# Layer 1's group norm through DRAM, and image 1's attention half by half, in a four-layer hybrid kernel

## The chip, the cores and the metric

One core of a Trainium2 chip runs the whole kernel in one launch. The metric is the device time of an execution in microseconds. PE is TensorE (matmuls), DVE VectorE, ACT ScalarE, POOL GpSimd, and SP the sequencer that issues most DMAs. Each engine works through its own queue in the order in which instructions stand in it; semaphores tie the queues together.

## The reference, cut to what matters

The input x is (2, 256, 32, 32), float32: two images of 1024 positions with 256 channels. Four layers follow; the change concerns the first two and the seams behind them.

```python
# layer 0: group norm with 32 groups, then attention of all 2048 positions, 4 heads
x = x + conv_attn(gn(x, G=32))
# layer 1: mean and variance of a WHOLE image, then attention inside the image, 8 heads of 64
mu  = mean(x, axis=(1, 2, 3)); var = var(x, axis=(1, 2, 3))
xn  = (x - mu) * rsqrt(var + 1e-5) * gn_w + gn_b
q, k, v = split(w_in @ xn)
x = w_out @ softmax(q * 0.125 @ k.T) @ v + b_out + x
# layer 2: tokens; layer norm, window attention (64 tokens, shifted), then layer norm, top-2 of 8 experts
t = tokens(x); t = t + window_attn(ln(t)); t = t + experts(ln(t))
# layer 3: layer norm, additive attention sum_u wa[u] * tanh(q + k + bh), then layer norm, top-2 of 8 experts
```

## The kernel before, in words

The state `xT` lies in SBUF as channels by positions (128 partitions, 2 halves of the channels, 2048 positions).

`project0` makes layer 0's queries, keys and values in four quarters of 512 positions (t = 0 to 3). At t = 0 and t = 2 it takes an image's group norm first: `group_norm` runs `bn_stats` on DVE, and `pool_stats` averages over partitions with small matmuls (L542 here), twice, for the mean and for the variance. `rsqrt` is a chain of twelve tiny DVE operations (L131 to L138), with no table.

`front` runs layers 0 and 1. It makes a list of chunks and hands it to `attention`. A chunk is 512 query positions of one pair of heads. Layer 0 has 8 chunks of 64 steps, layer 1 has 16 of 8 steps: for each image four pairs of heads, and for each pair two halves t of the positions. One step handles 128 keys: four pairs of score matmuls (L215, L216), one exp on ACT (L218) into one of four `e` buffers, one addition on DVE (L224, L227) for the softmax's denominator, and eight matmuls with the values (L237). The order of the program is written out by hand: `attention` scores one or two steps ahead, and hangs further work on step numbers in `todo`: `divide` two steps after a chunk's end (L251 to L265: the sums over partitions, a reciprocal, and the product that goes to `oT`), the chunk's `finish` four or six steps after it, the next chunk's `prepare` four steps before its start, and `extras` where a chunk names them. A scheduler in the framework may then move an instruction within its engine's queue where dependences allow, so a place in the program is not yet a place in the queue.

Around the change the order is this. `norm(b)` is layer 1's group norm of image b: `group_norm` with matmuls against a constant 1/256 (L410), then four passes over the image on DVE for `xn`. `values` (L432, L436) and `heads` (L446, L450) project from `xn`; `heads(b, pair)` makes the queries and keys of a pair for all 1024 positions. For image 0 these stand in the extras of layer 0's second half, four steps apart from step 8 of its fifth chunk on; for image 1 they stand in the late chunks of image 0's layer 1. The last chunk of an image calls `output1(b)` (32 matmuls L457, additions to `xT` L463) and then `done(b)`: the positions are transposed to tokens (L1432), copied (L1435, L1437), and normalised by `norms`: statistics of eight tokens' tiles (L144, L145), one `rsqrt`, the scaling on ACT (L155), and `to_channels` (transposes L182, copies L184, L186). For image 0 that falls into image 1's first chunks; for image 1 it is followed by the window attention (projections L684, L689, L696, scores L711).

The experts of layer 2 (`mixture`: products L1130, L1154, transposes L1141, gelu L1146) are a generator, `second`, stepped one block at a time. Between it and the additive attention stands `prepare(0, ...)`, a generator that brings in the experts' results of image 0 for each token tile (DMAs L1200 on the SP and ACT queues, combination L1202), then layer-norms them and makes the additive attention's first operands (L1251). `second` is stepped beside it from its ninth item on.

Of the kernel before, what the change touches and what calls it, by code (L numbers as in the profile page):

```python
# [24 lines left out]
F32 = mybir.dt.float32  # L25
# [3 lines left out]
AF = mybir.ActivationFunctionType  # L29
ALU = mybir.AluOpType  # L30
# [3 lines left out]
P = 128  # L34
B, C, N = 2, 256, 1024
# [52 lines left out]
class Stack:  # L88
# [101 lines left out]
    def attention(self, chunks, pools):  # L190
# [94 lines left out]
        for n in range(at + 5):  # L285
            ahead = 2 if 0 < n < at and steps[n][1] == 0 else 1
            while scored < min(n + ahead + 1, at):
                score(scored)
                scored += 1
            if n < at:  # L290
                accumulate(n)
            for f in todo.pop(n, []):
                f()
# [39 lines left out]
    def front(self, xT, weights, tokens, done):  # L333
# [6 lines left out]
        with ExitStack() as ctx:  # L340
# [61 lines left out]
            whole = w1.tile([P, P], F32, name="whole")  # L402
            nc.gpsimd.memset(whole, 1.0 / C)
            xn, v, oT, q, k = {}, {}, {}, {}, {}

            def norm(b):

                mean, rs = self.group_norm(
                    w1, p_r, xT, b, lambda ps, rows: [
                        nc.tensor.matmul(  # L410
                            ps[:, o : o + 1], lhsT=whole, rhs=rows[:, c : c + 1],
                            start=(c == 0), stop=(c == CC - 1),
                        )
                        for o in range(CC) for c in range(CC)
                    ]
                )
                xn[b] = pools1[0].tile([P, CC, N], F32, name="xn")
                for c in range(CC):
                    nc.vector.tensor_scalar(
                        xn[b][:, c, :], xT[:, c, b * N : (b + 1) * N],  # L420
                        mean[:, c : c + 1], rs[:, c : c + 1], ALU.subtract, ALU.mult,
                    )
                    nc.vector.tensor_scalar(
                        xn[b][:, c, :], xn[b][:, c, :], gn_w[:, c : c + 1], gn_b[:, c : c + 1],
                        ALU.mult, ALU.add,
                    )
                v[b] = pools1[b].tile([P, N // P, HID], F32, name="v")
# [10 lines left out]
            def heads(b, pair):  # L438

                for part, to, scale in ((0, q, 0.125), (1, k, 1.0)):  # L440
                    to[b, pair] = two.tile([P, N], F32, name="qh" if part == 0 else "kh")
                    for t in range(N // CH):
                        ps = bank()
                        for c in range(CC):
                            at = part * HID + pair * P
                            nc.tensor.matmul(  # L446
                                ps, lhsT=w_in[:, c, at : at + P], rhs=xn[b][:, c, t * CH : (t + 1) * CH],
                                start=(c == 0), stop=(c == CC - 1),
                            )
                        nc.scalar.activation(to[b, pair][:, t * CH : (t + 1) * CH], ps, AF.Copy, scale=scale)  # L450

            def output1(b):
                for t in range(N // CH):
                    for o in range(CC):
                        ps = bank()
                        for c in range(PAIRS):
                            nc.tensor.matmul(  # L457
                                ps, lhsT=w_out[:, c, o * P : (o + 1) * P],
                                rhs=oT[b][:, c, t * CH : (t + 1) * CH],
                                start=(c == 0), stop=(c == PAIRS - 1),  # L460
                            )
                        x = xT[:, o, b * N + t * CH : b * N + (t + 1) * CH]
                        nc.vector.scalar_tensor_tensor(x, ps, b_out[:, o : o + 1], x, ALU.add, ALU.add)  # L463

            def chunk1(b, pair, t):
                def prepare():
                    if t == 0 and pair:
                        heads(b, pair)

                def finish():  # L470
                    if pair == PAIRS - 1 and t == N // CH - 1:
                        output1(b)
                        done(b, bank)

                def goes_to():
# [8 lines left out]
                    "q": lambda: q[b, pair][:, cols],  # L484
# [9 lines left out]
            chunks += [chunk1(b, p, t) for b in range(B) for p in range(PAIRS) for t in range(N // CH)]  # L494


            for b, at, first_step, apart in ((0, NCH, 8, 4), (1, NCH * CC + 5, N // P - 2, 1)):
                ready = [lambda b=b: norm(b), *(lambda b=b, i=i: values(b, i) for i in range(N // P))]
                ready += [lambda: None, lambda b=b: heads(b, 0)]
                for i, f in enumerate(ready):  # L500
                    step = first_step + apart * i
                    for c in chunks[at:]:
                        if step < c["n"]:
                            c.setdefault("extras", {}).setdefault(step, []).append(f)
                            break
                        step -= c["n"]
            self.attention(chunks, pools)

    def project0(self, pool, psum, xT, weights, to):
# [26 lines left out]
        for t in range(NCH):  # L536
            cols = slice(t * CH, (t + 1) * CH)
            if t % 2 == 0:
                b = t * CH // N
# [842 lines left out]
    def run(self):  # L1382
        tc, nc, ins = self.tc, self.nc, self.ins
        PER = N // P
        with ExitStack() as ctx:
            window = ExitStack()
            xw = window.enter_context(tc.tile_pool(name="wa_in", bufs=1, side="right"))
            with tc.tile_pool(name="xT", bufs=1, side="right") as xp:
# [19 lines left out]
                def norm(which, g, bank):  # L1408

                    tiles = slice(4 * g, 4 * g + 4)  # L1410
                    t, u, uT, mv = (have[n] for n in ("t", "u", "uT", "mv"))
                    rs = self.normalise(u[:, tiles], t[:, tiles], mv[:, which, tiles], 1e-5)
                    self.to_channels(uT[:, :, g * CH : (g + 1) * CH], u[:, tiles], bank)
                    return mv[:, which, tiles, 1], rs
# [12 lines left out]
                def done(b, bank):  # L1427

                    for i in range(b * PER, (b + 1) * PER):
                        ps = bank(0)[:, 0:C].rearrange("p (c d) -> p c d", c=CC)  # L1430
                        for c in range(CC):
                            nc.tensor.transpose(ps[:, c, :], xT[:, c, i * P : (i + 1) * P], self.ident)  # L1432
                        to = have["t"][:, i, :].rearrange("p (c d) -> p c d", c=CC)
                        if i % 2:
                            nc.scalar.copy(to, ps)  # L1435
                        else:
                            nc.vector.tensor_copy(to, ps)  # L1437
                    norms(0, b, bank)
# [126 lines left out]
            with ExitStack() as side:  # L1565
# [18 lines left out]
                for k, _ in enumerate(prepare(0, bank, enter(side, "outputs2"), PER, nc.sync, nc.scalar)):  # L1584
                    if k >= PER:
                        second.step()
# [45 lines left out]
class General(Stack):  # L1632
# [4 lines left out]
    def front(self, xT, weights, tokens, done):  # L1637
# [4 lines left out]
        with self.tc.tile_pool(name="tok_ps", bufs=4, space=PSUM) as psum:  # L1642
            for b in range(B):
                done(b, lambda k: psum.tile([P, CH], F32, name="tr"))
# [543 lines left out]
```

## Time and profile before

| | |
|---|---|
| three runs | 2504.87, 2511.28, 2515.06 us; median 2511.28 |
| the profiled execution | 2506.88 us, its span 2504.9, mean PE clock 0.978 |
| layer 0's projections | about 0 to 70 us of the span |
| layer 0's attention, 8 chunks | 70 to 1016 |
| layer 1, image 0 | 1016 to 1184 |
| layer 1, image 1, with image 0's output and layer norm | 1184 to 1352 |
| image 1's output and layer norm | 1352 to 1386 |
| window attention, routing, layer 2's experts | 1386 to 1710 |
| seam to the additive attention, then that attention | 1710 to 2245 |
| layer 3's experts | 2245 to 2505 |

The page of a profile lists busy time and instructions by engine, the chain of work that ended last, and groups of instructions as "line engine operation out<-in, shapes, count | busy us, mean ns of one | idle time before them and what ended most of it". A timeline lists instructions by start (us), duration (us), engine, line and operation; in brackets the engine's idle time before it and what it waited for. "x8" joins neighbours of the same kind.

### The profile page before, as it was taken

How to read it: one execution, taken by the hardware profiler on the slowest of the kernel's cores; microseconds unless marked ns; L12 is line 12 of the kernel's file. 1: busy time of each engine (PE TensorE's matmuls, PEld its weight loads, DVE VectorE, ACT ScalarE, POOL GpSimd, SP SyncE). 2: the span in 40 equal slices, each digit the busy share in tenths (PEclk: the TensorE clock that was granted, in tenths of full speed). 3: DMA queues.
4: the chain of work that ended last, by engine and by line, in shares of the span. 5: the costliest groups of instructions: out<-in, count | busy, mean ns of one | idle time of the engine just before them, and what ended most of it. 6: DMA issues, size and time to landing. Idle time of an engine off the chain costs nothing.

```text
span 2504.9 us, 42385 instructions
## 1 busy us (share of the span) xinstructions
PE 2350.2 (94%) x17211; PEld 1024.5 (41%) x17211; DVE 1701.1 (68%) x2616; ACT 1436.9 (57%) x1626; POOL 241.6 (10%) x254
## 2 busy tenths in 40 slices
PE   7999999999999999999999969997999988889997
PEld 4333333333333333333333536664444432334664
DVE  5677777775677777876578566326877788886543
ACT  1565556545555566544454333222999999999222
POOL 0000000000000000000001312221110000111342
PEclk9999999999999999999999989998999999999998
DMA  4000000000000000000000036775343202122896
GB/s 139 1 1 1 1 1 1 1 1 1 1 1 1 1 2 1 1 1 1 1 2 9 3 117 244 297 289 208 137 141 136 90 14 78 66 91 93 305 323 236
DMA packets 58928, 190.50 MB, mean 76 GB/s; under 512 B 14116, under 2 KB 28964, under 8 KB 48740
## 3 DMA queue, kind: packets, MB, share of 16 engines
q1 hardware_dynamic: 45236, 161.86, 18.3%
q0 software_dynamic: 8160, 22.29, 2.5%
q10 hardware_dynamic: 5328, 3.55, 0.5%
q8 instruction: 137, 2.24, 0.4%
q14 instruction: 67, 0.55, 0.1%
HBM read 168.15 MB, written 17.43 MB: 74 GB/s over the span
## 4 chain that ended last, share of the span: by engine, by line
PE 70%; DVE 11%; issue 7%; ACT 6%; DMA 3%; POOL 1%; SPq 0%; ACTq 0%; DVEq 0%; POOLq 0%
PE ps_o L237 20%; PE ps_t L215 19%; PE ps_e L1304 7%; PE bk_h L1130 4%; PE bk_y L1154 4%; ACT th L1295 3%; DVE sum L227 2%; PE ps_row L446 2%; PE ps_pt L1325 2%; DVE th L1285 2%; PE ps_qk L530 1%; PE ps_row L432 1%; DVE den L263 1%; DMA w<-in_l_w 1%; PE ps_row L457 1%
## 5 line engine op out<-in xcount | busy, mean ns | idle before, releaser
L227 DVE TENSOR_TENSOR sum<-sum,e 128x1024 f32<-128x1024 f32 x592 | 724.9, 1224 | 303.5 <-ACT e L218 292.6
L218 ACT ACTIVATE e<-ps_t 128x1024 f32<-128x1024 f32 x640 | 653.4, 1025 | 464.9 <-PE ps_t L216 463.4
L237 PE MATMUL ps_o<-e,v 64*64 64x512 f32 x5120 | 677.0, 592 | 8.5 <-DVE o L244 7.9
L215 PE MATMUL ps_t<-q,k 64*64 64x512 f32 x2048 | 533.0, 591 | 0.5 <-DVE v L571 0.5
L216 PE MATMUL ps_t<-q,k 64*64 64x512 f32 x2048 | 533.0, 591 | 0.0
L1285 DVE TENSOR_SCALAR th<-kT,qb 128x1024 f32<-128x1024 f32 x478 | 331.2, 749 | 90.2 <-PE ps_e L1304 87.9
L237 PEld LDWEIGHTS ps_o<-e,v 64*64 64x64 f32 x5120 | 194.1, 132 | 370.8 <-issue 179.4
L1295 ACT ACTIVATE th<-th 128x4096 f32<-128x4096 f32 x94 | 335.8, 3651 | 5.2 <-DVE th L1285 5.2
L1146 ACT ACTIVATE h<-bk_t,w 128x128 f32<-128x128 f32 x496 | 142.5, 375 | 267.2 <-issue 149.8
L1304 PE MATMUL ps_e<-th,pick 128*32 128x512 f32 x2048 | 270.2, 621 | 25.4 <-ACT p L1357 15.0
L215 PEld LDWEIGHTS ps_t<-q,k 64*64 64x64 f32 x2048 | 149.2, 133 | 287.2 <-issue 152.9
L1130 PE MATMUL bk_h<-w,xgT 128*128 128x512 f32 x496 | 242.9, 606 | 10.3 <-DVE xgT L1118 9.9
L1154 PE MATMUL bk_y<-w,h 128*128 128x256 f32 x992 | 247.9, 385 | 3.0 <-issue 1.0
L1154 PEld LDWEIGHTS bk_y<-w,h 128*128 128x128 f32 x992 | 178.3, 192 | 48.7 <-issue 24.0
L1135 DVE COPY hp<-bk_h 128x512 f32<-128x512 f32 x124 | 85.3, 688 | 121.6 <-PE bk_h L1130 121.5
L265 POOL TENSOR_TENSOR inverses<-inverses,den 128x512 f32<-128x512 f32 x24 | 30.5, 1269 | 1325.0 <-DVE den L263 1325.0
L216 PEld LDWEIGHTS ps_t<-q,k 64*64 64x64 f32 x2048 | 149.3, 133 | 0.0
L215 PE MATMUL ps_t<-qh,kh 64*64 64x512 f32 x512 | 139.4, 602 | 0.0
L216 PE MATMUL ps_t<-qh,kh 64*64 64x512 f32 x512 | 138.5, 600 | 0.0
L1304 PEld LDWEIGHTS ps_e<-th,pick 128*32 128x32 f32 x2048 | 58.3, 112 | 172.0 <-issue 115.2
L1161 POOL DMA_INDIRECT given<-y,gives x85 | 87.0, 1023 | 428.8 <-DVE y L1160 358.4
L1130 PEld LDWEIGHTS bk_h<-w,xgT 128*128 128x128 f32 x496 | 86.9, 193 | 80.8 <-issue 54.8
(335 smaller groups left out, 2053.6 us busy)
## 6 DMA issues: line engine op xcount, KB each, us to landing
w<-in_l_w SPq DMA_DIRECT2D x39, 1152.0 KB, 5.4
w<-in_l_w SPq DMA_DIRECT2D x39, 1030.0 KB, 7.0
w<-in_l_w SPq DMA_DIRECT2D x46, 640.0 KB, 6.7
w<-in_l_w SPq DMA_DIRECT2D x46, 514.0 KB, 5.4
rows<-u SPq DMA_DIRECT2D x8, 512.0 KB, 3.7
yt<-given SPq DMA_DIRECT2D x24, 128.0 KB, 2.3
k<-k SPq DMA_DIRECT2D x16, 128.0 KB, 2.2
uT<-given ACTq DMA_DIRECT2D x16, 128.0 KB, 4.1
```

The lines of the kernel that those rows point to most:

```text
L215: nc.tensor.matmul(ps[part, 0, :], lhsT=ka[:, part], rhs=q[0:64, :], start=True, stop=True)
L216: nc.tensor.matmul(ps[part, 1, :], lhsT=kb[:, part], rhs=q[64:128, :], start=True, stop=True)
L218: nc.scalar.activation(e, ps, AF.Exp)
L227: nc.vector.tensor_tensor(c["sum"], c["sum"], e, ALU.add)
L237: nc.tensor.matmul(c["po"][64 * r : 64 * r + 64, half, :], lhsT=v[part, :], rhs=e[part, r, :], start=(j == 0), stop=(j == c["n"] - 1),)
L1130: nc.tensor.matmul(ps, lhsT=inputs[b][:, c, :], rhs=first[b][:, at : at + CH], start=(c == 0), stop=(c == CC - 1),)
L1146: nc.scalar.activation(hidden[b, n][:, cols], ps[:, cols], AF.Gelu, bias=first[b][:, at : at + 1])
L1154: nc.tensor.matmul(sums[b], lhsT=h[:, j * P : (j + 1) * P], rhs=second[b][:, at : at + C], start=(n == 0 and j == 0), stop=(n == HH - 1 an ...
L1161: nc.gpsimd.indirect_dma_start(out=given[b], out_offset=index(slots(b)[1], b), in_=y, in_offset=None)
L1285: nc.vector.tensor_scalar(h[:, j, :], *keys_and_queries(n, j), None, ALU.add)
L1295: nc.scalar.activation(h, h, AF.Tanh)
L1304: nc.tensor.matmul(scored[i][U * j : U * (j + 1), a, :], lhsT=aa["pick"][:, m, :], rhs=h[:, j, a * CH : (a + 1) * CH], start=(m == 0), sto ...
```

## The change

Five edits. (1) Image b's group norm in layer 1 no longer uses matmuls. `look(b)` takes the statistics of each channel with `bn_stats`, stores them (128 x 4 numbers) to DRAM, and loads the whole row back into every partition, into the space of `v[b]`, which is not yet in use. `norm(b)` combines them there with `bn_stats` again. `look` stands in the program eight steps (image 0), and some chunks (image 1), ahead of `norm`. (2) Image 1's chunks run half by half: the four pairs for the first 512 positions, then the four for the second. Keys of all four pairs are kept, those of pairs 2 and 3 in the space of image 0's values. (3) `output1` and `done` work on 512 positions, and return lists of small steps that `attention` hangs on successive step numbers; the layer norm's scaling moves from ACT to DVE. (4) `project0` takes image 1's group norm at t = 1, not t = 2. (5) `second` is stepped once more, at `prepare`'s third item. The diff, cut to its core:

```diff
@@ attention
-        for n in range(at + 5):
+        n = 0
+        while n < at or todo:
...
             for f in todo.pop(n, []):
-                f()
+                for i, g in enumerate(f() or []):
+                    later(n + 1 + i, g)
+            n += 1
@@ front
+            def look(b):
+                st = w1.tile([P, CC, 2, 6], F32, name="gn_st")
+                mv = w1.tile([P, CC, 2], F32, name="gn_mv")
+                for c in range(CC):
+                    for i in range(N // CH):
+                        at = b * N + i * CH
+                        nc.vector.bn_stats(st[:, c, i, :], xT[:, c, at : at + CH])
+                    nc.vector.bn_aggr(mv[:, c, :], st[:, c])
+                rows = self.tc.dram_tile([P, CC * 2], F32, name=f"gn_rows{b}")
+                nc.sync.dma_start(out=rows[:, :], in_=mv.rearrange("p c s -> p (c s)"))
+                v[b] = pools1[b].tile([P, N // P, HID], F32, name="v")
+                every = v[b][:, 0, 0 : P * CC * 2]
+                nc.sync.dma_start(out=every, in_=rows[:, :].rearrange("p x -> (p x)").partition_broadcast(P))
+
             def norm(b):
-                mean, rs = self.group_norm(
-                    w1, p_r, xT, b, lambda ps, rows: [
-                        nc.tensor.matmul(
-                            ps[:, o : o + 1], lhsT=whole, rhs=rows[:, c : c + 1],
...
+                every = v[b][:, 0, 0 : P * CC * 2].rearrange("p (c s) -> p c s", s=2)
+                for i in range(2):
+                    nc.vector.bn_stats(st[:, i, :], every[:, :, i])
+                    nc.vector.bn_aggr(mv[:, i, :], st[:, i])
+                var = w1.tile([P, 1], F32, name="gn_var")
+                nc.vector.tensor_tensor(var, mv[:, 0, 1:2], mv[:, 1, 0:1], ALU.add)
+                mean, rs = mv[:, 0, 0:1], self.rsqrt(var, 1e-5)
...
+            def heads(b, pair, t):
+                for i in (t,) if b else range(0 if t else N // CH):
+                    q[b, pair, i] = two.tile([P, CH], F32, name="qh", bufs=4)
+                    project(b, pair, 0, i, q[b, pair, i])
+                if t:
+                    return
+                if b and pair >= 2:
+                    if not spare:
+                        spare.append(pools1[0].tile([P, N // P, HID], F32, name="v"))
+                    at = (pair - 2) * (N // CH)
+                    k[b, pair] = spare[0][:, at : at + N // CH, :].rearrange("p a d -> p (a d)")
+                else:
+                    k[b, pair] = two.tile([P, N], F32, name="kh")
+                for i in range(N // CH):
+                    project(b, pair, 1, i, k[b, pair][:, i * CH : (i + 1) * CH])
...
                 def finish():
-                    if pair == PAIRS - 1 and t == N // CH - 1:
-                        output1(b)
-                        done(b, bank)
+                    if pair == PAIRS - 1 and (b or t):
+                        follow = []
+                        for i in (t,) if b else (0, 1):
+                            follow += [lambda i=i, o=o: output1(b, i, o) for o in range(CC)]
+                            follow += done(b * (N // CH) + i, bank)
+                        return follow
...
-            chunks += [chunk1(b, p, t) for b in range(B) for p in range(PAIRS) for t in range(N // CH)]
+            chunks += [chunk1(0, p, t) for p in range(PAIRS) for t in range(N // CH)]
+            chunks += [chunk1(1, p, t) for t in range(N // CH) for p in range(PAIRS)]
...
-            for b, at, first_step, apart in ((0, NCH, 8, 4), (1, NCH * CC + 5, N // P - 2, 1)):
+            for b, looked, at, first_step, apart in ((0, (NCH, 8), NCH, 16, 4), (1, (NCH * CC, 12), NCH * CC + 5, N // P - 2, 1)):
+                due(*looked, lambda b=b: look(b))
@@ project0
-            if t % 2 == 0:
-                b = t * CH // N
+            if t < B:
+                b = t
@@ run
+                def token(i, bank):
+                    ps = bank(0)[:, 0:C].rearrange("p (c d) -> p c d", c=CC)
+                    for c in range(CC):
+                        nc.tensor.transpose(ps[:, c, :], xT[:, c, i * P : (i + 1) * P], self.ident)
...
+                    stats(0, i)
+
+                def done(g, bank):
+                    tiles = [lambda i=i: token(i, bank) for i in range(4 * g, 4 * g + 4)]
+                    return [*tiles, lambda: norm(0, g, None), *3 * [lambda: None], lambda: turns(g, bank)]
...
                 for k, _ in enumerate(prepare(0, bank, enter(side, "outputs2"), PER, nc.sync, nc.scalar)):
-                    if k >= PER:
+                    if k == 2 or k >= PER:
                         second.step()
```

`due(at, step, f)` hangs f on a step of a chunk, carrying over into later chunks. `norm(0, g, None)` is the layer norm of four token tiles, scaled on DVE (L160), and `turns` its `to_channels`.

## The prediction

> **What bounds the kernel now.** I read the page's busy shares first, then the chain that ended last, then tables of busy time by stage, then the timeline at the places that the diff touches. TensorE carries the kernel:
>
> ```profile
> PE 2350.2 (94%) x17211; PEld 1024.5 (41%) x17211; DVE 1701.1 (68%) x2616; ACT 1436.9 (57%) x1626; POOL 241.6 (10%) x254
> ...
> PE 70%; DVE 11%; issue 7%; ACT 6%; DMA 3%; POOL 1%; SPq 0%; ACTq 0%; DVEq 0%; POOLq 0%
> ...
> L227 DVE TENSOR_TENSOR sum<-sum,e 128x1024 f32<-128x1024 f32 x592 | 724.9, 1224 | 303.5 <-ACT e L218 292.6
> ```
>
> PE is busy 94%, so an edit pays only where it closes one of PE's few gaps; removed work on DVE or ACT pays nothing by itself. In the attention loop one step costs PE 1.72 us (the distance of two exps in a quiet stretch, 1109.39 to 1111.11), ACT 1.02, and DVE 1.22 for L227. DVE thus has only 0.5 us per step to spare: that is the resource to watch. The exps in the timeline show what image 0's norm costs:
>
> ```profile
> 531.53 1.02 ACT L218 ACTIVATE e<-ps_t 128x1024 f32<-128x1024 f32 x1 [0.69 <-PE ps_t L216]
> 539.26 1.02 ACT L218 ACTIVATE e<-ps_t 128x1024 f32<-128x1024 f32 x1 [6.71 <-PE ps_t L216]
> 542.47 1.02 ACT L218 ACTIVATE e<-ps_t 128x1024 f32<-128x1024 f32 x1 [2.18 <-PE ps_t L216]
> ```
>
> Two steps took 10.94 us instead of 3.44: 7.5 us lost. The table by stage (window, then PE, PEld, DVE, ACT and POOL busy, PE clock, DMA share, GB/s) shows the other places: image 0's output and layer norm inside image 1's first chunks (row 1), the tail before the window attention (row 2), and the gap ahead of the additive attention (rows 3 and 4):
>
> ```profile
> 1184.00:1230.00 46.00, 43.46 (x199) 16.36 (x198) 26.63 (x54) 16.16 (x26) 1.27 (x1) 0.93 0.00 0
> ...
> 1352.00:1386.50 34.50, 29.40 (x105) 14.54 (x106) 24.71 (x61) 10.72 (x22) 13.41 (x24) 0.95 0.11 17
> 1710.00:1720.00 10.00, 3.81 (x16) 2.29 (x14) 4.24 (x12) 0.37 (x1) 0.96 (x1) 0.81 0.64 203
> 1720.00:1730.00 10.00, 4.34 (x8) 2.05 (x9) 10.00 (x51) 2.03 (x7) 0.99 (x1) 0.50 0.58 195
> ```
>
> **What the Trainium skill says.** (1) "DMA: Bandwidth & Descriptors", Anatomy of one DMA: about 2 us of every DMA is fixed, mostly the receipt of the last write. The trace agrees: a 0.1 KB load takes 1.7 to 1.8 us to land, one of 128 KB 2.2 to 2.9. (2) "TensorE: Matmul & The Clock Gate", Part 1: an idle window drops PE to half clock until about 3.4 us of work have passed. The trace agrees: after the stall at 535 a score matmul took 1.06 us, not 0.59, until 541. (3) Same page, Architectural detail: DVE is strict FIFO, so an instruction waiting for a DMA holds all behind it. The trace has one such wait in the attention stages, 3.8 us of L797 on `sb_rel_pos` at 1311, and does not contradict it. (4) "SBUF — State Buffer", Who interferes with whom: a DVE instruction with two SBUF inputs contends with a GpSimd read. The trace agrees: between 1374 and 1379 eight tiny ops of `rsqrt` took 0.65 us each instead of 0.17 while POOL ran L647.
>
> **A. Image 0's norm.** Removed: 16 L410 matmuls over both images (0.97 us for eight, two lots per image) and the `gs` chain between. Added: `look` (same bn_stats), a store of 2 KB, a broadcast load of 256 KB, then bn_stats on the loaded rows and `rsqrt`, all DVE. Price of the exchange: 1.8 + 2.3 (an `out` store of 256 KB) plus two issues of 0.3 = 4.7 us; bounds 4.0 (1.7 + 2.2) and 6.2 (2.9 + 2.9 + issue). The program puts `look` eight steps ahead of `norm` (13.7 us), which would hide it. But in the built order of the queues the scheduler has moved `norm`'s first bn_stats up to only two L227 sums behind `look`'s last. Data ready at 532.3, landed near 537; DVE arrives there near 534.8 and waits some 2.3 us, with the sums queued behind it. `e` has four buffers, so the exps, and then PE, run dry: I count about 3.8 us of PE stall plus 1.2 of lowered clock. 7.5 - 5.0 = **2.5 gained**. Bounds: exchange at 4.0, 6 gained; at 6.2, 2 lost.
>
> **B. Image 1's norm.** Exps at 1111.11, 1116.71 and 1119.62 today: 5.07 us too much, 5.5 with the xn wait. Afterwards its statistics are taken at layer 1's first chunk near 1018, where `norm`'s wait is again pulled close behind. DVE then runs 4.7 us late, but there PE does 7.1 us of head projections and DVE idles 4.5 us, which hides it with about 1 us to spare. **5.5 gained**; 1 if the exchange takes 6.2 or that cover is thinner.
>
> **C. Image 1 half by half, layer norm in steps.** Today from the first L457 product of image 0 (1184.01) to the first window score (L711, 1386.06): 202 us, made of 168.5 to the last L251 (1352.47) and a tail of 33.6. Of the 168.5, PE has 151.7 of work: 60 steps x 1.72 = 103, L251 8, heads 21.2, output 13.9, transposes 5.6; the rest, 16.8, is stall.
>
> The tail's lines, with their waits:
>
> ```profile
> 1353.48 14.00 PE L457 MATMUL ps_row<-oT,sb_l_w_out 128*128 128x512 f32 x32
> 1354.44 3.36 DVE L263 RECIPROCAL den<-total 128x256 f32<-128x256 f32 x2 [0.69 <-ACT total L257]
> ...
> 1380.34 4.04 ACT L155 ACTIVATE u<-t,nm_shift,rs 128x256 f32<-128x256 f32 x8 [4.20 <-DVE nm_shift L153]
> 1380.99 0.33 PE L182 MATMUL ps_row<-ident,u 128*128 128x128 f32 x1 [3.01 <-ACT u L155]
> ```
>
> After: only half of the 32 L457 products, four tokens instead of eight. L251 to oT 7 us (as now, 1352.47 to 1359.49), last two products and add 1.7, four tokens at 1.0 (transposes 0.34, copy 0.41, bn_stats 0.42), `rsqrt` 12 x 0.19 = 2.3, L160 4 x 0.41 = 1.6, transposes and copies 2; with 1.4 of chunk ends, **20**. The window projection of image 0 (16 x 0.43 = 6.9) fills PE during this. Bounds: 18.5, and 26 if POOL's L647 adds fall on `rsqrt` again (12 x 0.48 more).
>
> The stretch before it grows. PE takes over 8.8 us from the tail (160.5). DVE now owes each group of four tokens about 9.5 us (copies 0.8, bn_stats and aggregates 2.4, `rsqrt` 2.5, L160 1.6, uT copy 0.7, output adds 1.5) over 15.2 per chunk (8 x 1.22, o copies, reciprocal 3.4, L264): 24.7 against 22.6 for a PE chunk with its heads. So DVE is just over PE: about 3 us in each of three groups, plus 3 once where the single `oT` buffer makes DVE's L264 wait for the products that still read it: stalls 12. 160.5 + 12 + 20 = 192.5; say 194 for clock loss. **8 gained**; bounds 14 (stalls halved) and 2 lost (DVE 5 us more per group).
>
> **D. project0.** The gap at 35.33 (PE waits 3.37 for xn, then 5.28 for eight matmuls instead of 3.43) is moved up a quarter, not covered: L542 is queued right behind quarter 0's values, and image 1's bn_stats run only after quarter 0's value adds on DVE. **0** (-2 to +2). The k writes on SP are 128 KB each and follow; nothing waits for them before 70 us.
>
> **E. One expert block more ahead of the additive attention.** PE waits 7.2 us there on L1146, which is queued behind L1200's DMA issues on ACT, and 4.6 on L1118, behind L1202 on DVE. After: three L1200 issues, one more, then L1146, so part of 7.2 goes; and one block's 2.3 us of gelu and 8 us of PE leave the additive stage, where ACT is busy 484 of 505 us. Against it, that block stands before the chain that starts this stage: 3 us later. **1 gained** (-4 to +5).
>
> SP's queue gains four DMAs; the last also waits for the old readers of its buffer, but SP has nothing else to issue until the tail. POOL is untouched.
>
> **Sum:** 2.5 + 5.5 + 8 + 0 + 1 = 17. The profiled execution took 2506.88 (span 2504.9), so 2490; it lies 4.4 below the median of the three runs, 2511.28, so on that footing **2494**. A measurement of this kernel can tell about 0.5% from no change: 12.6 us.
>
> **Rivals.** *All hidden as the program intends*: the scheduler's order costs nothing since the DMA lands in 4 us; A 6, B 5.5, C 14, D 2, E 4: 31.5, giving 2480. For it: DVE is idle a third of the time. Against: the queue order. *Gains eaten by DVE*: the bound in C moves to DVE (24.7 against 22.6 leaves no margin) and A nets nothing; 5.5 + 0 = 2506. For it: L244's waits of up to 1.2 us on PE already occur today. *Slower*: the wait at the exchange is longer. From about 8 us (two DMAs at twice today's latency, because the broadcast's 128 reads of one 2 KB row queue) each further us is paid by PE in A, and in B once 1 us of slack is gone; at 15 us A costs 8 net and B 4; with C at its 2 and E at its 4 this is 18 lost, 2529. Against it: DMA engines stand idle there (DMA share 0.00 to 0.01). *The lead does not exist*: "ahead of time" holds in the program but not on the queues; this is my forecast's own assumption for A, and if it is wrong, the first rival's 6 stands there.
>
> **Numbers.** As summed, 0.60 (three quarters of it beyond 12.6 us): faster 0.45, same 0.15. All hidden 0.17. Eaten 0.16: 0.02 faster, 0.14 same. Slower 0.07. Together 0.64, 0.29, 0.07. Range: low 2474 (all hidden with the runs' own spread of 5), high 2513 (gains eaten, with the same spread).
>
> **What would show it.** No L410 at 532 or 1112; DVE idle ahead of the new bn_stats near 535 (2 to 3 us) with a PE gap of about 4, near 1018 DVE idle without one. Time from image 0's first output product to the first window score 192 to 197, its tail 20. PE's gap in project0 near 25 instead of 35. PE's 7.2 us on L1146 gone or halved. I am wrong if DVE's wait at 535 is nil, if image 1's chunks of 8 steps exceed 29 us, or if the additive stage starts over 5 us late.

## The result, and the profile after

The changed kernel takes 2499.47 us (median of 17 runs, 2493.68 to 2507.79); the kernel before, on the same chips, 2508.30 (17 runs, 2502.01 to 2515.06). The ratio is 0.9966, 95% interval 0.9955 to 0.9977: 8.5 us less, between 5.8 and 11.3. The forecast was 17 us less with a range that holds this result; but a gain of over 0.5% was given 0.64, and what came is within 0.5%. The profiled execution after took 2503.26 us, its span 2501.5, so that one lies 3.8 above the median of its runs, where the profiled run before lay 1.4 below its own: the two profiles differ by only 3.6 us, and I read them by stage, not by their ends.

Busy shares and the chain that ended last, from the page of the kernel after:

```profile
PE 2349.4 (94%) x17179; PEld 1019.2 (41%) x17179; DVE 1711.1 (68%) x2656; ACT 1428.4 (57%) x1610; POOL 241.6 (10%) x253
...
PE 71%; DVE 10%; issue 7%; ACT 6%; DMA 4%; POOL 1%; SPq 0%; ACTq 0%; DVEq 0%; POOLq 0%
```

As before: PE sets the time, and the averages say nothing of the change. The stages do. I lay the two profiles over each other by the n-th instruction of a kind (n-th exp of the attention loop, first window score, n-th gelu, first tanh). The column says how much earlier (-) the kernel after is than the kernel before at that mark:

| mark | earlier by, us |
|---|---|
| first exp (after `project0`) | +1.1 |
| 315th exp (image 0's norm and projections done) | -2.8 |
| 563rd exp (image 1's norm done) | -8.5 |
| last L251 of layer 1 | -5.0 |
| first window score | -13.6 |
| first gelu of layer 2's experts | -11.9 |
| 89th gelu | -6.5 |
| first L1200 DMA of the seam (L1239 after) | -10.2 |
| first tanh of the additive attention | -5.2 |
| end | -3.4 |

So the front of the kernel gained 14.7 us from the first exp to the window attention, close to what the forecast summed, and then gave part of it back. In the lines below the timeline's columns are start, duration, engine, line and operation, with the idle time before it and its cause in brackets. Image 0's norm, first ACT's exps and then DVE:

```profile
539.52 1.02 ACT L218 ACTIVATE e<-ps_t 128x1024 f32<-128x1024 f32 x1 [0.69 <-PE ps_t L216]
542.63 1.02 ACT L218 ACTIVATE e<-ps_t 128x1024 f32<-128x1024 f32 x1 [2.08 <-DVE rs L138]
546.71 1.02 ACT L218 ACTIVATE e<-ps_t 128x1024 f32<-128x1024 f32 x1 [3.05 <-DVE sum L227]
```

```profile
533.36 2.50 DVE L227 TENSOR_TENSOR sum<-sum,e 128x1024 f32<-128x1024 f32 x2
538.64 0.75 DVE L431 BATCH_NORM_STATS2 gn_all<-v 128x6 f32<-128x256 f32 x2 [2.78 <-DMA v<-gn_rows]
...
1018.25 0.75 DVE L431 BATCH_NORM_STATS2 gn_all<-v 128x6 f32<-128x256 f32 x2 [3.29 <-DMA v<-gn_rows]
```

The bn_stats of `norm` stand two sums behind `look`, and DVE waits 2.78 us there with the sums behind it; the data arrive 5.2 us after the last statistic (533.44 to 538.64). Two exps later the exps themselves wait for DVE to free an `e` buffer. At 1018 DVE waits 3.29 us for image 1's exchange, and no exp is late: PE is in the head projections. The tail, on PE and DVE:

```profile
1364.11 0.69 DVE L131 TENSOR_SCALAR rs<-mv 128x4 f32<-128x4 f32 x1
...
1366.19 0.64 DVE L136 TENSOR_TENSOR rs<-rs 128x4 f32<-128x4 f32 x1
...
1366.87 0.65 DVE L137 TENSOR_TENSOR rs<-rs 128x4 f32<-128x4 f32 x1
1367.55 0.65 DVE L138 SCALAR_TENSOR_TENSOR rs<-rs 128x4 f32<-128x4 f32 x1
...
1369.42 2.20 DVE L160 TENSOR_SCALAR u<-t,mv,rs 128x256 f32<-128x256 f32 x4
1369.91 2.98 POOL L686 TENSOR_TENSOR t<-t,sb_wa_b_out 128x256 f32<-128x256 f32 x4 [1.72 <-DVE u L160]
1369.97 0.71 PE L182 MATMUL ps_row<-ident,u 128*128 128x128 f32 x2 [4.05 <-DVE u L160]
```

The four slow operations of `rsqrt` and the slow L160 fall on POOL's L686 additions (L647 before). The tail, from the first matmul of the last L251 (1347.48) to the first window score (1372.51), takes 25.0 us against 33.6. In the seam (columns as in the forecast's table by stage) PE is busier than before in both windows, though these are the same times and not quite the same work, since the seam starts 10.2 us earlier; over the whole seam, first L1200 DMA to first tanh, PE is busy 30.1 of 38.4 us against 21.0 of 33.5:

```profile
1710.00:1720.00 10.00, 7.80 (x20) 4.39 (x18) 7.08 (x23) 0.88 (x3) 0.99 (x1) 0.66 0.91 304
1720.00:1730.00 10.00, 7.42 (x31) 4.38 (x32) 8.61 (x42) 2.79 (x9) 1.96 (x2) 1.00 0.63 228
```

### The profile page after: what moved, and what is told of

The parts are those of the page before. It is cut to its first block, busy times and chain, and to the rows that moved or that the text cites. A ratio compares the mean times of both kernels' runs of the same rounds, so it can differ in the third digit from the quotient of the medians.

```text
span 2501.5 us, 42355 instructions
## 1 busy us (share of the span) xinstructions
PE 2349.4 (94%) x17179; PEld 1019.2 (41%) x17179; DVE 1711.1 (68%) x2656; ACT 1428.4 (57%) x1610; POOL 241.6 (10%) x253
## 4 chain that ended last, share of the span: by engine, by line
PE 71%; DVE 10%; issue 7%; ACT 6%; DMA 4%; POOL 1%; SPq 0%; ACTq 0%; DVEq 0%; POOLq 0%
PE ps_o L237 20%; PE ps_t L215 20%; PE ps_e L1343 6%; PE bk_h L1169 5%; PE bk_y L1193 5%; ACT th L1334 3%; PE ps_row L460 2%; DVE th L1324 2%; DVE sum L227 2%; PE ps_pt L1364 2%; DMA w<-in_l_w 1%; PE ps_qk L569 1%; PE ps_row L450 1%; PE ps_row L489 1%; PE bk_t L1180 1%
## 5 line engine op out<-in xcount | busy, mean ns | idle before, releaser
L237 PE MATMUL ps_o<-e,v 64*64 64x512 f32 x5120 | 663.3, 590 | 10.7 <-DVE o L244 7.2
L1200 POOL DMA_INDIRECT given<-y,gives x85 | 86.7, 1020 | 459.5 <-DVE y L1199 386.3
L1140 POOL DMA_INDIRECT xg<-rows,takes x85 | 88.6, 1043 | 273.8 <-PE bk_x L1152 224.2
L215 PE MATMUL ps_t<-qh,kh 64*64 64x512 f32 x384 | 98.7, 598 | 0.0
```

Of the source, the lines that this page charges most:

```text
L215: nc.tensor.matmul(ps[part, 0, :], lhsT=ka[:, part], rhs=q[0:64, :], start=True, stop=True)
L237: nc.tensor.matmul(c["po"][64 * r : 64 * r + 64, half, :], lhsT=v[part, :], rhs=e[part, r, :], start=(j == 0), stop=(j == c["n"] - 1),)
L1140: nc.gpsimd.indirect_dma_start(out=tokens[b], out_offset=None, in_=rows(b)[:, :], in_offset=index(slots(b)[0], b))
```

## The experiments

Twelve kernels were timed beside the kernel before, in five rounds each (6 to 22 executions of each; six for e9 and e11, seven for e12). "Front" is how much earlier the first window score comes than in the profile before, counted from the first exp, so that the start's own scatter (-0.3 to +2.1 us over all profiles) drops out. It is from one profile each and scatters by some 2 us: e2, whose front is unedited, shows +3.3. "Whole" is the ratio and what it makes of 2508: the median of many runs, where "front" is one profile.

| kernel | front, us | ratio (95%) | whole, us | exchange DMAs or scratch |
|---|---|---|---|---|
| the change | -14.7 | 0.9966 (0.9955 to 0.9977) | -8.5 | yes |
| e1, without the extra block | -14.2 | 0.9960 (0.9947 to 0.9972) | -10.0 | yes |
| e2, the extra block alone | +3.3 | 0.9998 (0.9987 to 1.0008) | -0.5 | no |
| e3, the norm alone | -7.3 | 0.9987 (0.9977 to 0.9997) | -3.3 | yes |
| e4, the halves alone | -6.1 | 0.9969 (0.9956 to 0.9983) | -7.8 | no |
| e5, image 0's norm pinned | -15.0 | 0.9959 (0.9949 to 0.9969) | -10.3 | yes |
| e6, an unused exchange | +0.3 | 1.0013 (1.0002 to 1.0024) | +3.3 | yes |
| e7, POOL's additions late | -16.2 | 0.9987 (0.9976 to 0.9999) | -3.3 | yes |
| e8, norm with no exchange | -3.9 | 0.9999 (0.9987 to 1.0011) | -0.3 | no |
| e9, one set of products | -12.8 | 0.9945 (0.9930 to 0.9960) | -13.8 | no |
| e10, e9 and two stores | -11.5 | 0.9980 (0.9970 to 0.9989) | -5.0 | scratch, stores |
| e11, e9 and four tiny loads | -12.8 | 0.9955 (0.9937 to 0.9973) | -11.3 | no |
| e12, e9 with ACT's copy | -14.7 | 0.9954 (0.9937 to 0.9971) | -11.5 | no |

**Is it the extra block at the seam? e1 and e2.**

```diff
-                    if k == 2 or k >= PER:     # e1: from the changed kernel; e2: the reverse, in the kernel before
+                    if k >= PER:
```

> The changed kernel without its last edit: second is no longer stepped at the third item of prepare. Theory 1 (the extra expert block in the seam costs): in the two profiles the changed kernel reaches the seam 10.2 us early and its first tanh only 5.2 us early, so without the block the first tanh should be 9 to 11 us ahead of the kernel before, and the time about 2495, ratio 0.994 to 0.995. Theory 2 (an early gain is absorbed anyway, in the experts and in the additive stage): the first tanh no more than 7 us ahead and the time as with the extra block, 2499, ratio 0.9965.

> The kernel before with the extra expert block at the seam alone. Theory 1: PE's wait of 7.2 us on the gelu goes, but the first tanh comes 3 to 6 us later than in the kernel before; the block saves some of it later, so the time is 0 to 4 us above the kernel before (ratio 1.000 to 1.002). Theory 2: no effect on the first tanh beyond 1 us; the time within 1 us. My prediction had 1 us gained.

From the seam's first L1200 DMA to the first tanh it takes 33.5 us in the kernel before and 37.6 in e2, 34.8 in e1 and 38.4 in the changed kernel: the block does delay the additive attention, by some 4 us. But the whole cannot be told apart with and without it in either surrounding (0.9960 against 0.9966, and 0.9998, each to some 3 us): the block is moved and not added, and what it takes here it no longer takes elsewhere. Theory 1 was right on the delay and wrong on its price: the edit is worth nothing that can be measured, and the loss is elsewhere.

**The norm alone and the halves alone: e3 and e4.** e3 puts `look`, the new `norm` and `due` into the kernel before; e4 takes the changed kernel and puts back the norm by products, t = 0 and 2 in `project0`, and the old seam.

> The kernel before with layer 1's norm through DRAM alone, chunks and layer norms as before. The profiles put the norm's gain at 4.0 us (image 0) and 5.7 us (image 1), so the first window score should come 9 to 10 us early. If an early gain is carried to the end: 2498.5, ratio 0.996. If it is absorbed later: 2502 to 2505, ratio 0.998 to 0.999.

> The kernel before with image 1's chunks half by half and the layer norm in steps alone (norm by products, project0 and the seam as before). From the profiles: from image 0's first output product to the first window score 5 us less (189.5 lengthened by 4 before the last sum over partitions and shortened by 9 after it), so the first window score 5 us early. If it is carried: 2503, ratio 0.998. If absorbed: 2506 to 2508, ratio 0.999 to 1.000.

By the medians of the runs the halves keep what they gain: 6.1 at the front, 7.8 at the end (interval 4.3 to 11.0). The norm does not: the last L251 is 9.1 us earlier, the first window score 7.3, the end 3.3 (0.8 to 5.8). That points to the norm as the place of the loss and does not prove it: by the ends of these two profiles alone, each counted from its first exp, e3 keeps 5.1 of its 7.3 and e4 only 2.9 of its 6.1.

**Does the wait for the exchange cost, or DVE's own work? e5.**

```diff
+            self.last_e = e                    # in score()
...
+                if b == 0:                     # in norm(), ahead of its bn_stats
+                    nc.gpsimd.tensor_copy(st[:, :, 0], self.last_e[:, 0, 0:2])
```

> The changed kernel with one edit: a tiny POOL copy ties image 0's norm to the exp of the step at which the program places it, so that its bn_stats stand eight sums later in DVE's queue, after the exchange has landed. Theory 1 (A's remaining cost is the wait for the exchange): DVE's idle time of 2.78 us ahead of that bn_stats goes and PE gets it back: the norm's stretch of layer 0's fifth chunk 2.5 to 3.5 us shorter than in the changed kernel. Theory 2 (the cost is DVE's own burst: bn_stats, rsqrt and four passes for xn, some 6.7 us that exceed what four e buffers cover): the wait goes but PE still stalls, the stretch less than 1 us shorter. The total should move by no more than these, 2496.5 to 2499.5.

DVE's bn_stats now come without a wait, and the exps run on undisturbed for some eight steps more (ACT's timeline of e5, then DVE's, then PE's):

```profile
550.20 1.02 ACT L218 ACTIVATE e<-ps_t 128x1024 f32<-128x1024 f32 x1 [0.69 <-DVE rs L137]
551.96 1.02 ACT L218 ACTIVATE e<-ps_t 128x1024 f32<-128x1024 f32 x1 [0.74 <-DVE rs L138]
556.33 0.58 ACT L457 COPY v<-ps_row 128x512 f32<-128x512 f32 x1 [3.35 <-PE ps_row L453]
557.38 1.02 ACT L218 ACTIVATE e<-ps_t 128x1024 f32<-128x1024 f32 x1 [0.46 <-PE ps_t L216]
```

```profile
547.41 0.76 DVE L434 BATCH_NORM_STATS2 gn_all<-v 128x6 f32<-128x256 f32 x2
...
552.00 1.53 DVE L441 TENSOR_SCALAR xn<-xT,gn_both,rs 128x1024 f32<-128x1024 f32 x2
553.45 1.53 DVE L445 TENSOR_SCALAR xn<-xn,sb_gn_w,sb_gn_b 128x1024 f32<-128x1024 f32 x2
554.89 5.21 DVE L228 TENSOR_TENSOR sum<-sum,e 128x1024 f32<-128x1024 f32 x4
```

```profile
554.31 1.98 PE L453 MATMUL ps_row<-sb_l_w_in,xn 128*128 128x512 f32 x4 [1.61 <-DVE xn L445]
```

Yet there is a stall. The exps at 551.96 and 557.38 are 5.42 apart, with a value projection between them; the next such pairs (562.53 to 566.32, and every fourth after that) are 3.79 apart. So 1.6 us are lost, and PE's line shows them: it waits 1.61 us for `xn`, the end of DVE's block of `rsqrt` and `xn`. At the 315th exp e5 is 5.8 us ahead of the kernel before and the change 4.0, each counted from its first exp. Of the 7.5 us that the norm cost before, the change thus still pays 3.5: about 1.9 for the wait, and 1.6 for DVE's own block. Each theory had part of it. The ratio (0.9959) does not tell e5 from the change.

**Why is the norm's gain lost? e6, e8.** e6 adds to the kernel before a store and a broadcast load for each image, with no reader. e8 is e3 with the two DMAs taken out and `norm` reading its own partition's statistics.

```diff
+            def exchange(b):                   # e6, hung on a step of its own
+                rows = self.tc.dram_tile([P, CC * 2], F32, name=f"gn_rows{b}")
+                nc.sync.dma_start(out=rows[:, :], in_=whole[:, 0 : CC * 2])
+                v[b] = pools1[b].tile([P, N // P, HID], F32, name="v")
+                every = v[b][:, 0, 0 : P * CC * 2]
+                nc.sync.dma_start(out=every, in_=rows[:, :].rearrange("p x -> (p x)").partition_broadcast(P))
```

> The kernel before with the four DMAs of the exchange added (the store of 2 KB and the load of 256 KB for each image, at the places of the changed kernel) and nobody waiting for them before the values are written; the norm still comes from products. It asks why the norm alone (9 us earlier at the front) brought only 2.7 at the end, with the experts' first blocks 5 us longer in its profile. Theory 1 (the DMAs themselves shift what comes later, through the place of other scratch in DRAM or through the order of the DMA queues' completion): the experts' stretch from first to 89th gelu is 99 to 100 us instead of 94.7, and the time 2511 to 2514. Theory 2 (the experts' weight loads land early or late by chance and the loss has nothing to do with the norm): 2507 to 2510, the stretch 95 to 97.

> The kernel before with layer 1's norm computed without products and without any exchange: each partition normalises by the mean and variance of its own two channels (this leaves the averaging over partitions out, so it is another computation), look and norm at the places of the changed kernel. No DMA is added and nothing is waited for. At the front I expect what the norm alone brought, 7 to 9 us, plus some 2 to 3 us of DVE's wait, so the first window score 9 to 12 us early. Theory 1 (the exchange's DMAs cost some 3 us later in the kernel): the whole gain arrives, ratio 0.995 to 0.9965, about 2498. Theory 2 (half of any gain at the front is lost in the experts and the additive stage, which have waits of their own): ratio 0.9975 to 0.9985, 2503 to 2505.

Four DMAs that nobody waits for, at a place where DMA engines idle, make the kernel 3.3 us slower, interval 0.5 to 6.0. The front is unchanged (+0.3). The experts' stretch (first to 89th gelu), though, is 95.9 us, as theory 2 had it; the loss shows in no single stage of that one profile. e8 missed on both theories, since its front gained only 3.9: without the wait, `norm`'s operations fall between two other groups of DVE work at layer 1's start, and the 524th exp loses 4.8 us there. From a front so small little can be told, but as far as it goes it speaks against the exchange: e8 has none, and its whole is 3.6 us short of its front, as e3's is by 4.0.

**One set of products instead of the exchange: e9, and e12.** From the changed kernel without the extra block:

```diff
-                rows = self.tc.dram_tile(...); two DMAs; bn_stats of the loaded rows in norm
+                # in look: sq = (mean, var + mean * mean) of each channel
+                ps = bank()
+                for c in range(CC):
+                    nc.tensor.matmul(ps[:, 0:2], lhsT=whole, rhs=sq[:, c, :], start=(c == 0), stop=(c == CC - 1))
+                nc.vector.tensor_copy(both[b], ps[:, 0:2])      # e12: nc.scalar.copy
+                # in norm: var = both[1] - both[0] ** 2, then rsqrt
```

> The changed kernel without the extra expert block, and with the exchange through DRAM replaced by one set of products in look: mean and mean square of each channel, two matmuls of two columns against the constant 1/256, copied out, and combined on DVE in norm. PE pays 0.5 us for two matmuls per image and waits for nothing; DVE waits for no DMA. Against the changed kernel the front gains the 2 to 3 us of DVE's wait at image 0. Theory 1 (the exchange's DMAs cost later): ratio to the kernel before 0.993 to 0.9945, 2491 to 2495, faster than both. Theory 2 (half is absorbed later): 0.9955 to 0.9965, no better than the changed kernel.

> The kernel e9_one_product with the copy of the products' sum on ACT instead of DVE. In e9 PE waits 2.52 us at 1022.8 for a bank of ps_row that this copy holds, because DVE comes to it only behind a reciprocal and two sums, and the 523rd to 526th exp lose 4.9 us. Theory 1: those 4 to 5 us return, the first window score 16 to 18 us early, ratio 0.992 to 0.993, about 2490. Theory 2 (DVE's lateness from rsqrt is what costs): 0 to 1.5 us return.

e9 gains less at the front than the change, 12.8 us, and more at the end, 13.8: ratio 0.9945, the lowest ratio measured here (its interval, up to 0.9960, overlaps a little with the change's, from 0.9955, and more with e1's, from 0.9947). Its front loses 4.9 us at layer 1's start (at the 527th exp), where PE waits for the bank that DVE's late copy holds (PE's timeline of e9):

```profile
1025.36 7.12 PE L462 MATMUL ps_row<-xn,sb_l_w_in 128*128 128x512 f32 x12 [2.52 <-DVE gn_both L429]
```

Only 2.5 of the 4.9 are the wait. Most of the rest is clock: these twelve products take 7.12 us at a mean granted clock of 0.76, as long as sixteen take in the kernel after (7.13). With the copy on ACT (e12) 4.5 of these come back by the 556th exp, but the first window score is 14.7 us early, not 16 to 18, and the whole is no better than e9. The mechanism at that place was right; it did not reach the end, and why was not found.

**Which part of the exchange? e10, e11.** e10 adds to e9 the two scratch tiles and their stores; e11 adds four loads of one number each and no scratch.

```diff
+                rows = self.tc.dram_tile([P, CC * 2], F32, name=f"gn_rows{b}")                   # e10
+                nc.sync.dma_start(out=rows[:, :], in_=mv.rearrange("p c s -> p (c s)"))
...
+                for z in range(2):                                                               # e11
+                    nc.sync.dma_start(out=w1.tile([1, 1], F32, name=f"tiny{b}{z}"), in_=self.ins["ba"].unsqueeze(0))
```

> The kernel e9_one_product with two DRAM scratch tiles of 2 KB added, each stored to once by SP in look and read by nobody. e9 arrives 12.8 us early at the window and ends 13.8 us early; kernels with the exchange lose 4 to 6 us on the way. Theory 1a (the scratch in DRAM shifts the place of the experts' rows and slows their weight loads): the experts' stretch from first to 89th gelu 97 to 100 us instead of 95.3, the ratio 0.9955 to 0.9965. Theory 1b (it is the broadcast loads or SP's order): as e9, 95 to 96 us and 0.994 to 0.995.

> The kernel e9_one_product with four loads of one number each on SP's queue in look, with no scratch in DRAM and no reader; SP has as many DMAs as in the changed kernel, so each later DMA stands four places on in the round of completion semaphores. Theory 1b (the order of SP's DMAs and their semaphores): the experts' stretch 97 to 100 us, ratio 0.9955 to 0.9965. Theory 1a (scratch in DRAM): as e9, 95 to 96 us, 0.994 to 0.995. If both this and the stores are as e9, neither is the cause.

Two stores of 2 KB that nobody reads take e9 from 0.9945 to 0.9980, and the intervals do not meet: 8.8 us between the middles. e9 ran on another chip than e10, each beside the kernel before; on e10's own chip the two kernels without scratch, e11 and e12, stand at 0.9955 and 0.9954, some 6.3 us below it, and their intervals meet e10's only at the edge (0.9970). Four loads of one number (e11) are not told apart from e9. So a number of DMAs on SP's queue does not appear to be the cause; of the kernels compared, it is the one with scratch in DRAM and writes to it that is slower.

How the loss comes about is not shown. e10's experts' stretch is 96.4 us, below what theory 1a gave, while its ratio is worse than that theory allowed. Behind the first window score e10's profile is 5.6 us longer than e9's, and that is spread: 1.6 us to the first gelu, 1.1 to the 89th, 1.2 to the seam, -0.2 in it, 1.2 to the last tanh, 0.7 to the end. No single stage holds it. Nor do all kernels divide cleanly. Whole less front is +3.0 to +6.5 us in the seven with scratch, -3.8 to +3.6 in the other six (means 4.8 and 0.3; e7 counted from its last window score, since its edit lengthens the window attention): the ranges overlap, for e12 and e8, without scratch, lie at 3.2 and 3.6.

One rival stands untested: the granted clock. In the kernel before, a run is some 1.5 to 2.6 us longer for each 0.001 that its mean clock is lower (straight lines through 19 to 46 runs on four chips). e9's six runs lie at 0.9785 on average and e10's 22 at 0.9758, while the kernel before lay at 0.9757 and 0.9765 beside them. By those slopes, as an estimate, 4 to 7 of the 8.8 us go with the lower clock. Whether the stores change where the clock falls, or stalls come first and the clock falls behind them as at 1025 in e9, the record does not say.

**Why is the tail 25 us? e7.**

```diff
+            late = w.tile([P, C], F32, name="b_late")
+            nc.vector.tensor_copy(late[:, 0:1], uT[:, 1, T - 1 : T])   # not before the last uT
-            nc.vector.tensor_tensor(b_out, b_out, ps, ALU.add)
-            for i in range(NT):
-                nc.gpsimd.tensor_tensor(t[:, i, :], t[:, i, :], b_out, ALU.add)
+            nc.vector.tensor_tensor(late, b_out, ps, ALU.add)          # and one addition ahead of each values(i)
```

> The changed kernel with POOL's sixteen additions of the window attention's bias (L686) held until the last uT and emitted tile by tile. Theory 1 (the tail is 24.5 us instead of my 20 because those additions run beside rsqrt and L160 on DVE): rsqrt's operations at 0.16 to 0.3 us again, from the last L251 to the first window score 20.5 to 22 us, and the window attention no longer. Theory 2 (the tail is PE's own work and other DVE work put in between): 24 us or more.

DVE's timeline of e7, and then PE's waits in its window attention (total, times, longest):

```profile
1363.69 0.16 DVE L138 SCALAR_TENSOR_TENSOR rs<-rs 128x4 f32<-128x4 f32 x1
...
1365.06 1.38 DVE L160 TENSOR_SCALAR u<-t,mv,rs 128x256 f32<-128x256 f32 x4
```

```profile
PE ps_av L779 <- POOL l L759: 7.6, 1, 7.6
```

With POOL quiet, `rsqrt` runs at 0.16 us an operation and L160 at 0.35 a tile, and DVE's stretch from the first of `rsqrt` to the end of L160 is 4.6 us instead of 7.5. The tail shrinks by only 1.8 us, to 23.2, between the two theories: in e7's queue four window projections (L723, 1.98 us) have slipped behind the last transposes, ahead of the first window score. And 1.8 is less than tails differ anyway: e4, e9 and e11 have 23.8 with POOL's additions where they were, e5 and e12 26.2 and 26.4. So the price of the contention is about 3 us on DVE and not measured apart in the whole. The additions then delay POOL's products in the window attention, where PE waits 7.6 us once for them; the whole is some 5 us worse than the change.

## Why the prediction was right or wrong

**A, image 0's norm: right in mechanism, 2.5 forecast, 4.0 measured** (first exp to 315th). The scheduler's pull is there, DVE waits 2.78 us (2.3 forecast), the exchange takes 5.2 us (4.7). The price, 5.0, was put wholly on the wait; 3.5 was paid, and e5 splits it: 1.9 for the wait, 1.6 for DVE's own block, which stalls PE even without a wait. The 1.2 us for a lowered clock did not come: the granted clock is 1.00 from 532 to 553. (The section that the forecast names from the Trainium skill, "DMA: Bandwidth & Descriptors", Anatomy of one DMA, describes DMAs issued by GpSimd; these go out from SP, and their price came from the trace.) The bound of 6 that the forecast gave for an exchange of 4.0 us is what came with no wait at all (5.8).

**B, image 1's norm: right.** 5.5 forecast, 5.6 measured (556th to 563rd exp), with DVE's wait of 3.29 us hidden behind the head projections as worked out.

**C, half by half: right in sign, 8 forecast, 5.1 measured.** The stretch to the last L251, counted from the 563rd exp, grew by 3.5 (4 forecast, and 1.5 for the clock). DVE's excess per chunk did not appear as forecast: PE's waits between 1176 and 1373 are three short lists,

```profile
PE ps_row L182 <- DVE u L160: 4.5, 3, 4.0
PE ps_o L237 <- DVE o L244: 2.9, 2, 1.9
PE ps_row L251 <- DVE sum L227: 2.7, 1, 2.7
```

of which the stretch has the last two. PE is idle 7.3 of its 232.8 us; before it was idle 10.4 of 229.3. So stalls shrank by 3 us, not by the 5 that I forecast, and PE's busy time grew by 6.6 instead of the 8.8 that moved in, at a granted clock of 1.00 instead of 0.99. The forecast's stalls were too large on both sides: of the 16.8 us before (1184 to 1352.5) PE was idle 9.1, and busy 159.4, not 151.7; waits for DVE of 3 us a group did not come, although DVE's list behind the 15.2 us a chunk adds up to some 16 (9.8, 1.3, 3.4, 1.8). The term that was mis-sized is the tail: 20 forecast, 25.0 measured. From L251 to oT it was 7.0, as forecast; the last products and their addition took 4.0 instead of 1.7, since PE came to them 1.4 us late, behind L680 and twelve earlier products that took 7.11 us; the tokens 5.6 instead of 4.0, with DVE's mask work (L700, L702) put in between; `rsqrt` 5.3 instead of 2.3; L160 2.2 instead of 1.6. I named POOL's additions as the upper bound of 26 and did not take it, although the profile before showed the same overlap. Two of the eight slow operations there (L133, L134), and L160 after, read one tensor and not two, so the forecast's reading by two inputs does not cover them; they slowed all the same. The twelve products are a matter of the clock: in e9 they take 5.42 us behind the same wait on L251 (kernel after, then e9),

```profile
1347.48 1.08 PE L251 MATMUL ps_row<-sum,ones 128*64 128x512 f32 x4 [2.67 <-DVE sum L227]
1348.49 7.11 PE L489 MATMUL ps_row<-oT,sb_l_w_out 128*128 128x512 f32 x12
...
1351.50 1.08 PE L251 MATMUL ps_row<-sum,ones 128*64 128x512 f32 x4 [2.68 <-DVE sum L227]
1352.51 5.42 PE L491 MATMUL ps_row<-oT,sb_l_w_out 128*128 128x512 f32 x12
```

at a granted clock of 0.76 in the first and 1.00 in the second, and that tail is 23.8 us. So about 1.2 of the 5 us missed is a lower clock that the same wait brings in one kernel and not in the other.

**D, project0: 0 forecast, 0.5 to 1.1 lost.** The gap moved as said, from 35 to 25; PE's two lines there are

```profile
29.25 0.56 PE L581 MATMUL ps_gs<-gn_mv,group 128*128 128x2 f32 x2 [3.44 <-DVE gn_mv L625]
...
31.15 5.42 PE L569 MATMUL ps_qk<-xn,sb_wk 128*128 128x512 f32 x8
```

The last quarter ends 1.13 us later; 0.5 of that is the gap (values to keys 5.5 us instead of 5.15, and a slower restart), the rest the first quarter's own slow start, which also varies between kernels whose start is the same.

**E, the extra block: 1 forecast, nothing measured** (e1, e2). Both halves of the sum were there: PE's wait of 7.2 us on the gelu is down to 0.8, and the seam is 4 us longer, 3 forecast.

**The step that failed, as far as the runs show, is the one that cost the exchange's DMAs nothing beyond the wait for them** ("SP has nothing else to issue until the tail"). The sum as a whole was 17 and 8.5 came. At the window attention it stood at 14.7 against a forecast of 16 for A to D, where A's surplus and C's shortfall partly cancelled, which is luck; at the end 8.5 was left. e6 (+3.3) and e10 (+8.8 against e9, 6.3 against e11 and e12) show a kernel with scratch in DRAM and stores to it to be slower, and not at the place of the stores; four loads without scratch (e11) are not measurably so. What carries the cost is open. In the profile after, DVE waits for the experts' weights longer than before in the first 89 gelus,

```profile
DVE xgT L1157 <- DMA w<-in_l_w: 7.0, 4, 2.4
```

against 3.4 us, for a weight load that was issued at the same distance from the first gelu (21.6 us) and whose reader could start 1.8 us later. But e12, without scratch, shows such a long stretch too (98.5 us), and e6 and e10 with scratch do not (95.9, 96.4). The long stretch is no accident of one profile, for e3, e5 and e7, which have the whole exchange, show it too (99.5 to 99.8 us, with DVE waiting 6.3 to 6.9 us for the weights; e1 97.0 and 5.2). So the late landings explain part of the change's loss, and not e10's. Whether the place of later scratch buffers in DRAM or the writes themselves do it was not tried, nor whether the clock carries it.

Of the rivals, "gains eaten by DVE" fell (the chunks are bound by PE), "slower" fell (the exchange took 5.2 us), and "all hidden" fell on A and on the tail; "the lead does not exist" held, since DVE waits 2.78 us, and the 6 that it set for A without that wait is what e5 shows. (The range's upper end, 2513, is 2 more than the 2506 and the spread of 5 that it is made of.) The result lies between the forecast and "eaten", for a reason that no rival named.

## What to carry to other kernels

A gain at the front of a long kernel has to be followed to the end by marks along the way: here the parts that were computed well at the front (14.7 of 16 us) were not what arrived (8.5). The exchange through DRAM brought less at the end than its latency and its wait account for, and a small set of products did the same work with a whole at least as good (e9's 0.9945 against e1's 0.9960, intervals overlapping), although PE waited 2.5 us for it at one place. Where a scheduler orders the queues, "ahead of time" in the program has to be looked up in the queue, and if need be held there by a dependence.

## What the runs showed of the hardware

With two stores of 2 KB to DRAM scratch that nobody reads, a kernel of 2495 us was some 8.8 us slower (6.3 against its two nearest relatives on one chip); with four loads of one number each it was not measurably slower. The way of the loss is open. A wait of 2.7 us on PE was followed by a granted clock of 0.76 over the next 7 us in one kernel and by 1.00 in another. Operations of `rsqrt` (128 x 4) and of L160 (128 x 256) on DVE took up to 0.69 us instead of 0.16 and 0.55 instead of 0.35 while POOL added tensors, and returned to the lower figures when POOL was kept quiet (e7). That took some 3 us off DVE's work and 1.8 off the tail, and the moved additions cost PE one wait of 7.6 us elsewhere.
